# Four chained image layers on one Trainium2 core: where the table switches of Gelu and Silu may stand among the scan steps, and where the A matrices are loaded

## Chip, core and metric

The kernel runs on one core of one Trainium2 chip. The metric is the device time of one execution in microseconds (us); the lower, the better. All data is 32-bit float.

## What is computed

Eight images of 56 x 56 pixels with 192 channels go through four layers. Layer 0 has a convolution branch on one half of the channels and a state-space branch on the other; layers 1 and 2 are state-space layers; layer 3 is windowed attention with an MLP. Cut to what matters here:

```python
# layer 0: left half                       # right half
xl = relu(conv1x1(conv3x3(conv3x3(xl))))   xz = layernorm(xr) @ in_proj
                                           u  = silu(depthwise3x3(xz[:192])); gate = silu(xz[192:])
# layers 0, 1, 2: for each of 4 directions k over the 3136 pixels
dts, B, C = split(x_proj[k] @ u)           # rank 6 or 12, 16, 16 rows
delta = softplus(dt_proj[k] @ dts + bias)
A = -exp(A_logs)                           # [4, 192, 16]
h = exp(delta[d] * A[d, n]) * h + delta[d] * u[d] * B[n]     # 192 x 16 states, one recurrence each
y[d] = sum_n h[d, n] * C[n]                # summed over directions, plus D * u; then a layernorm
# layer 3: 7x7 windows, 6 heads: attention, layernorm, x1; then
out = x1 + layernorm(gelu(x1 @ fc1 + b1) @ fc2 + b2)
```

## The kernel before, in words

**The scans.** A step is one recurrence of 128 rows (32 channels x 4 states) over 784 pixels. One pass of one direction over a quarter of an image is a unit of 24 steps: two channel halves of 12 steps, each 4 groups of states x 3 groups of channels. There are 8 images x 3 layers x 4 directions x 4 quarters = 384 units, so 9216 steps; an image has 1152. In step s the loop in `run` emits:

- on ScalarE the exponential of step s, `ps_x = exp(dsp * A)`, into one of two PSUM buffers (`make`); A is used as the scale, one column per step. Ahead of it stands a copy of the last column of step s-2 into `state`;
- on GpSimd the product `db = usp * bt` of step s;
- on VectorE the scan of step s-1 and, for three steps of four, the product with `ct` into `hc`. Where s-1 is 3 mod 4 the scan writes `hc` and GpSimd makes the product one step later, so VectorE has a shorter step and GpSimd a longer one;
- on TensorE, for every third step, the sums over states into `ps_y` (`add_up`). At s = 5 mod 12 the finished half is copied out of `ps_y` by ScalarE (`merge`).

**Work ahead and work beside.** Three queues of Python generators are polled at the end of each step; only the head of a queue runs, and a `yield n` makes it wait n steps. `ahead` holds `prepare`: for a half that starts 13 steps later it makes two matmuls into both spare PSUM banks, then the softplus on ScalarE (with `table_time` before it), a product on GpSimd and six loads through SyncE's DMA queue. `urgent` holds `after` and `columns` (layernorms and projections between layers). `back` holds, for each image in this order, `ssm_front` of the next image (7 bands, Silu), `attention_block` of the previous image (8 rows of windows, one Gelu each) and `conv_front` of the next. After the `ahead` queue is polled, pieces of `urgent` and then of `back` are emitted as long as a budget of TensorE and ScalarE time per step (`SPARE`, at most `MOST`) is positive. `need` runs all queues with `forced` set until a named piece is done; it is what runs the prologue. Two PSUM banks serve all of this work (`bank`, `all_banks`). Each engine runs its instructions in exactly the order in which they were emitted (`in_order`).

**Tables.** Softplus, Gelu and Silu each need another activation table than the exponentials. Each use is a table load, the function, and a load back (`use_ln_exp`, line 390). `table_time` (line 393) lets such a use in only at steps 1 or 2 mod 4, unless forced.

**A.** In `constants` (lines 252 to 270) each layer's A is fetched by 16 DMAs that GpSimd issues (line 264), then ScalarE takes the exponential (line 268) and VectorE the negative (line 269). The queue of SyncE carries nearly all other transfers.

Of the kernel before, what the change touches and what calls it, by code (L numbers as in the profile page):

```python
# [32 lines left out]
AF = mybir.ActivationFunctionType  # L33
# [19 lines left out]
NSG = N // SN  # L53
NG = C // G * NSG
# [84 lines left out]
class Net:  # L139
# [56 lines left out]
    def constants(self, ctx):  # L196
        nc, cp = self.nc, self.cp
        self.vt = self.const("vec", [CH, NV])
        self.ident = cp.tile([128, 128], F32, name="ident")
        make_identity(nc, self.ident)  # L200
        self.ones = cp.tile([CH, CH], F32, name="ones")
        nc.vector.memset(self.ones, 1.0)
        self.eps = cp.tile([128, 1], F32, name="eps")
        nc.vector.memset(self.eps, EPS)
        self.blk = self.const("blk", [CH, CH])
        self.esum = cp.tile([128, G], F32, name="esum")
        nc.vector.reduce_sum(
            self.esum, self.ident.rearrange("p (d n) -> p d n", n=SN), axis=AX.X
        )


        self.wx = []
        for l in range(3):
            R = RANK[l]
            wx = cp.tile([CH, 2, 2, 4 * N + 2 * R], F32, name=f"wx{l}")
            for k in range(K):
                d, at = k // 2, 4 * N + k // 2 * R
                src = self.a[f"wx{l}"][:, :, k, :]
                nc.sync.dma_start(
                    out=wx[:, :, k % 2, 2 * N * d : 2 * N * d + 2 * N], in_=src[:, :, R:]  # L220
                )
                nc.scalar.dma_start(out=wx[:, :, k % 2, at : at + R], in_=src[:, :, :R])
                for c in range(2):
                    at = VAT[f"dtb{l}"] + c * K + k
                    nc.gpsimd.dma_start(
                        out=self.dtw[:1, l, k, CH * c : CH * c + CH],
                        in_=self.a["vec"][:, at : at + 1].rearrange("p o -> o p"),
                    )
            self.wx.append(wx)
            nc.sync.dma_start(out=self.dtw[1 : 1 + R, l], in_=self.a[f"dtw{l}"])  # L230

        with self.tc.tile_pool(name="setup", bufs=1) as sp:

            rstd = sp.tile([CH, 3], F32, name="rstd")
            at = VAT["bn1_v"]
            nc.scalar.activation(rstd, self.vt[:, at : at + 3], AF.Sqrt, bias=self.eps[:CH])
            nc.vector.reciprocal(rstd, rstd)
            self.bns = cp.tile([CH, 3], F32, name="bns")
            self.bnb = cp.tile([CH, 3], F32, name="bnb")
            at = VAT["bn1_g"]  # L240
            nc.vector.tensor_mul(self.bns, self.vt[:, at : at + 3], rstd)
            t = sp.tile([CH, 3], F32, name="bnt")
            at = VAT["bn1_m"]
            nc.vector.tensor_copy(t, self.vt[:, at : at + 3])
            for i in (1, 2):
                nc.vector.tensor_sub(t[:, i : i + 1], t[:, i : i + 1], self.v(f"conv{i}_b"))
            nc.vector.tensor_mul(t, t, self.bns)
            at = VAT["bn1_b"]
            nc.vector.tensor_sub(self.bnb, self.vt[:, at : at + 3], t)


            self.dsum = dsum = cp.tile([CH, 3, 2], F32, name="dsum")
            self.A = []
            for l in range(3):
                at = VAT[f"D{l}"]
                d = self.vt[:, at : at + 2 * K].rearrange("p (c k) -> p c k", k=K)
                nc.vector.reduce_sum(dsum[:, l, :], d, axis=AX.X)
                A = cp.tile([128, K, C // G, NSG], F32, name=f"A{l}")
                src = self.a[f"A{l}"].rearrange(
                    "(d s n) (k j q) -> q s d n k j", s=NSG, n=SN, k=K, q=4  # L260
                )
                for q in range(4):
                    for sg in range(NSG):
                        nc.gpsimd.dma_start(
                            out=A[32 * q : 32 * q + 32, :, :, sg], in_=src[q, sg]
                        )
                A = A.rearrange("p k j s -> p (k j s)")
                nc.scalar.activation(A, A, AF.Exp)
                nc.vector.tensor_scalar_mul(A, A, -1.0)
                self.A.append(A)  # L270


            ls = sp.tile([CH, 2], F32, name="ls")
            at = VAT["ls"]
            nc.vector.tensor_scalar_min(ls, self.vt[:, at : at + 2], math.log(100.0))
            nc.scalar.activation(ls, ls, AF.Exp)
            self.scm = cp.tile([CH, 2, 3], F32, name="scm")
            at = VAT["hm"]
            for c in range(2):
                nc.vector.tensor_scalar_mul(  # L280
                    self.scm[:, c, :], self.vt[:, at : at + 3], ls[:, c : c + 1]
                )
            self.ln1024 = cp.tile([CH, 1], F32, name="ln1024")
            nc.vector.memset(self.ln1024, 10.0 * math.log(2.0))

    def l3_constants(self):

# [105 lines left out]
    def table_time(self):  # L393


        while self.step % 4 not in (1, 2) and not self.forced:
            yield 1

    def other_table(self, func, *tiles):
# [415 lines left out]
    def run(self):  # L815
        nc = self.nc
# [13 lines left out]
        for i in range(NC):  # L830
            self.urgent.append(Task(self.after(-1, i)))
        self.urgent.append(Task(self.columns(0)))
        self.state = self.s1.tile([128, NG], F32, name="state")
        self.B_, self.C_, self.spread = {}, {}, {}

# [2 lines left out]
        ]  # L838
        S = len(steps)
        half = NG // 2  # L840
        self.step = 0
        self.ahead.append(Task(self.prepare(units[0], 0, 0)))
        self.need(("half", 0))
        self.ahead.append(Task(self.prepare(units[0], 1, half)))
        for sg in range(NSG):
            self.load_bc(units[0], sg)
        made, weighed, copies = {}, {}, deque()
        left = dict.fromkeys(self.load, 0.0)
        for s in range(S + 8):
# [5 lines left out]
            t = s + half + 1  # L855
            if t < S and t % half == 0:
                self.ahead.append(Task(self.prepare(*steps[t][:2], t)))
            if s < S and s % half == 0:
                self.need(("half", s))
                U = steps[s][0]  # L860
                if s % (16 * NG) == 0:
                    if U.l == 0:
                        self.begin_image(U.b)
                    self.dd = self.s1.tile([CH, 2, CH], F32, name="dd")
                    for c in range(2):
                        nc.scalar.activation(
                            self.dd[:, c, :], self.ident[:CH, :CH], AF.Copy,
                            scale=self.dsum[:, U.l, c : c + 1],
                        )

            t = s - 2
            if 0 <= t < S and not steps[t][0].last:
                U, h, sg, j = steps[t]
# [5 lines left out]
            t = s - 1  # L879
            if 0 <= t < S:  # L880
                U, h, sg, j = steps[t]
                x, db = made[t]
                pool = t % 4 == 3
                hc = self.s6.tile([128, CK], F32, name="hc")
                hs = hc if pool else x
                sense = slice(None) if U.k < 2 else slice(None, None, -1)
                nc.vector.tensor_tensor_scan(
                    hs[:, sense], x[:, sense], db[:, sense],
                    0.0 if U.first else self.at_state(h, sg, j), ALU.mult, ALU.add,
                )  # L890
                if not pool:
                    nc.vector.tensor_mul(hc, hs, self.C_[U, sg])
                made[t] = hs
                weighed[t] = hc
            t = s - 2
            if 0 <= t < S and t % 4 == 3:
                U, h, sg, j = steps[t]
                nc.gpsimd.tensor_mul(weighed[t], weighed[t], self.C_[U, sg])
            t = s - 4
            if 0 <= t < S and t % 3 == 2:  # L900
                U, h, sg, j = steps[t]
# [6 lines left out]
            while self.piece(self.ahead):  # L908
                pass
            self.spend(left, before)  # L910
            for queue in (self.urgent, self.back):
                while min(left["PE"], left["ACT"]) > 0.0 and self.piece(queue):
                    before = self.spend(left, before)

            t = s - 4
            if 0 <= t < S and t % NG >= half and t % 3 == 2:
                n = t // NG + 1
# [484 lines left out]
MOST = {"PE": 3.4, "ACT": 2.5, "DVE": 1.6, "POOL": 3.0}  # L1402


def view(t, k, c, i, n):

    if k % 2 == 0:
        return t[:, c, i : i + n]
    return t.rearrange("p c (h w) -> p c w h", w=HW)[:, c, i // HW : (i + n) // HW, :]
# [120 lines left out]
```

## Time and profile before

| | |
|---|---|
| median of 3 runs | 27071.03 us (27067.4 to 27074.87) |
| the profiled execution, its own time | 27060.61 us |
| its span, first to last instruction | 27058.8 us |
| VectorE (DVE) busy | 24122.4 us, 89% |
| GpSimd (POOL) busy | 23054.4 us, 85% |
| ScalarE (ACT) busy | 17211.8 us, 64% |
| TensorE (PE) busy | 18495.3 us, 68% |
| table loads | 1793 of 1.283 us |

Lines of the profile name engine, operation, output and input tiles, count, busy time and the idle time before the instructions with what ended it. Where the order was written out by hand most instructions carry line 109, so tiles tell them apart: `ps_x<-dsp,A` is a step's exponential, `TENSOR_TENSOR_SCAN` its scan, `db<-usp,bt` GpSimd's product, `delta<-ps_p` the softplus, `hid<-hid` the Gelu, `uband<-uband` and `sz<-sz` the Silu, `act<-ps_y` the merge copy. A line `ACT_TABLE_LOAD` with L109 or L268 goes to another table, one with L390 back.

### The profile page before, as it was taken

To read this page: it belongs to the slowest core of one execution; us is meant where nothing else is said; L and a number is where in the kernel's file an instruction comes from. 1 tells how busy PE (TensorE), PEld (TensorE's weight loads), DVE (VectorE), ACT (ScalarE), POOL (GpSimd) and SP (SyncE) were. 2 spreads that over 40 slices of the span, in tenths; PEclk is the share of its full clock that TensorE was granted. 3 is DMA by queue.
4 is the path that set the end of the run, shared out by engine and by line. 5 is a ranking of instruction groups with operands and counts; after the bars stand their busy time and mean duration, and the time that the engine had idled before them with its cause. 6 is when DMAs were issued, how large, how long until landed. Compare 5 with 4: busy or idle time off the path is not lost. (4 is left out here: it accounts for less than half of the span.)

```text
span 27058.8 us, 260255 instructions
## 1 busy us (share of the span) xinstructions
PE 18495.3 (68%) x76788; PEld 6432.0 (24%) x76788; DVE 24122.4 (89%) x18972; ACT 17211.8 (64%) x30893; POOL 23054.4 (85%) x13199
## 2 busy tenths in 40 slices
PE   6675567676676666766667676677766776676657
PEld 2221122222222222222222222222212222222114
DVE  5999999999999899999999999989999899999991
ACT  4655566665666666666666666666666666666655
POOL 5888988888888888888888888888888888888991
PEclk7776677777777777777777777777777777777777
DMA  4555565556555565555655556555565555555550
GB/s 96 135 138 124 133 136 133 126 127 139 135 132 127 125 144 132 132 126 129 142 131 132 127 131 140 133 129 127 131 140 131 129 128 135 134 129 129 130 132 25
DMA packets 1503447, 3472.21 MB, mean 128 GB/s; under 512 B 310618, under 2 KB 503219, under 8 KB 1502020
## 3 DMA queue, kind: packets, MB, share of 16 engines
q1 hardware_dynamic: 1496452, 3455.15, 56.0%
q8 instruction: 606, 9.93, 0.1%
q0 software_dynamic: 3072, 0.31, 0.1%
q14 instruction: 821, 6.73, 0.1%
q10 hardware_dynamic: 2496, 0.09, 0.0%
HBM read 1457.23 MB, written 147.89 MB: 59 GB/s over the span
## 5 line engine op out<-in xcount | busy, mean ns | idle before, releaser
L109 POOL TENSOR_TENSOR db<-usp,bt 128x784 f32<-128x784 f32 x9216 | 16832.7, 1857 | 161.8 <-DMA usp<-du 129.3
L109 DVE TENSOR_TENSOR_SCAN ps_x<-ps_x,state,db 128x784 f32<-128x784 f32 x5184 | 9569.7, 1846 | 834.0 <-ACT state L109 358.7
L109 ACT ACTIVATE ps_x<-dsp,A 128x784 f32<-128x784 f32 x9216 | 8464.1, 919 | 2496.9 <-DVE hc L109 2190.5
L109 PE MATMUL ps_y<-hc,esum 128*32 128x392 f32 x36864 | 6959.3, 641 | 1147.3 <-POOL hc L109 780.6
L109 DVE TENSOR_TENSOR hc<-ps_x,ct 128x784 f32<-128x784 f32 x6912 | 6739.5, 975 | 651.4 <-DVE ps_x L109 11.0
L109 POOL TENSOR_TENSOR hc<-hc,ct 128x784 f32<-128x784 f32 x2304 | 4254.4, 1847 | 2696.2 <-ACT state L109 2104.5
L109 ACT COPY state<-ps_x 128x1 f32<-128x1 f32 x5184 | 831.4, 160 | 4659.5 <-DVE hc L109 4637.4
L109 DVE TENSOR_TENSOR_SCAN hc<-ps_x,state,db 128x784 f32<-128x784 f32 x1728 | 3181.7, 1841 | 161.6 <-POOL db L109 58.2
L109 DVE TENSOR_TENSOR_SCAN ps_x<-ps_x,db 128x784 f32<-128x784 f32 x1728 | 3085.0, 1785 | 261.1 <-ACT state L109 149.1
L109 PEld LDWEIGHTS ps_y<-hc,esum 128*32 128x32 f32 x36864 | 1630.6, 130 | 6096.7 <-issue 3212.3
L109 PE MATMUL ps_y<-act,ident 96*96 96x392 f32 x2304 | 1612.2, 835 | 1760.4 <-ACT act L109 1746.4
L109 PE MATMUL ps_p<-act,act 13*96 13x392 f32 (+1 forms) x3072 | 1513.0, 605 | 1116.6 <-ACT s L109 210.4
L109 POOL TENSOR_TENSOR du<-delta,act 96x784 f32<-96x784 f32 x768 | 1567.9, 2042 | 201.3 <-ACT delta L109 198.7
L109 PE MATMUL ps_p<-act,wx 96*88 96x392 f32 (+1 forms) x1536 | 985.8, 778 | 686.9 <-ACT delta L109 394.0
L109 ACT ACT_TABLE_LOAD x896 | 1149.6, 1283 | 34.4 <-PE ps_p L109 18.9
L390 ACT ACT_TABLE_LOAD x897 | 1150.9, 1283 | 15.6
L109 PEld LDWEIGHTS ps_y<-act,ident 96*96 96x96 f32 x2304 | 465.0, 223 | 2603.1 <-ACT act L109 2056.6
L109 DVE TENSOR_TENSOR_SCAN hc<-ps_x,db 128x784 f32<-128x784 f32 x576 | 1025.8, 1781 | 58.8 <-ACT state L109 38.0
L109 PEld LDWEIGHTS ps_p<-act,act 13*96 13x96 f32 (+1 forms) x3072 | 465.4, 180 | 2033.6 <-issue 373.5
L109 ACT COPY act<-ps_y 96x784 f32<-96x784 f32 x768 | 928.0, 1208 | 8.5 <-PE ps_y L109 8.5
L109 PE MATMUL ps_p<-xip,diag 96*96 96x448 f32 x2016 | 864.0, 580 | 94.4 <-ACT delta L109 94.3
L109 ACT COPY state<-hc 128x1 f32<-128x1 f32 x1728 | 328.6, 190 | 883.6 <-DVE hc L109 880.4
(212 smaller groups left out, 18126.0 us busy)
## 6 DMA issues: line engine op xcount, KB each, us to landing
dsp<-delta SPq DMA_DIRECT2D x2304, 392.0 KB
usp<-du SPq DMA_DIRECT2D x2304, 392.0 KB
bt<-bcd SPq DMA_DIRECT2D x1536, 392.0 KB
ct<-bcd SPq DMA_DIRECT2D x1536, 392.0 KB
wf<-in_wf SPq DMA_DIRECT2D x128, 288.0 KB
wf<-wf2d SPq DMA_DIRECT2D x128, 288.0 KB
bcd<-bcx SPq DMA_DIRECT2D x256, 134.8 KB
szd<-sz SPq DMA_DIRECT2D x56, 336.0 KB
```

Source lines behind the costliest of these rows:

```text
L109: return call(out, *args, **k)
L390: self.tc.nc.scalar.preload_act_table_set(LN_EXP)
```

## The change

`table_time` now tells the softplus (queue `ahead`) from the others. Both still wait for steps at which neither this step nor the one before is 3 mod 4; beside that, nobody may start at 5 mod 12, and Gelu and Silu not at 0, 1 and 2 mod 12 either. So the softplus may stand at 1, 2, 6, 9 or 10 mod 12, Gelu and Silu at 6, 9 or 10. While a softplus waits, `urgent` and `back` emit nothing in that step (`quiet`); after a step in which Gelu or Silu waited, `back` is polled ahead of `urgent` (`wanted`). The A of layer 0 is fetched by ScalarE's DMA queue in the prologue, and its exponential comes after the first half has been prepared; those of layers 1 and 2 are fetched by SyncE and worked on in tasks at the end of the first `urgent` queue. `products` only gives a name to an expression that was there.

```diff
--- before.py
+++ after.py
@@ -250,24 +250,22 @@
 
 
             self.dsum = dsum = cp.tile([CH, 3, 2], F32, name="dsum")
-            self.A = []
+            self.A, self.logs = [], []
             for l in range(3):
                 at = VAT[f"D{l}"]
                 d = self.vt[:, at : at + 2 * K].rearrange("p (c k) -> p c k", k=K)
                 nc.vector.reduce_sum(dsum[:, l, :], d, axis=AX.X)
                 A = cp.tile([128, K, C // G, NSG], F32, name=f"A{l}")
+                self.A.append(A.rearrange("p k j s -> p (k j s)"))
                 src = self.a[f"A{l}"].rearrange(
                     "(d s n) (k j q) -> q s d n k j", s=NSG, n=SN, k=K, q=4
                 )
-                for q in range(4):
-                    for sg in range(NSG):
-                        nc.gpsimd.dma_start(
-                            out=A[32 * q : 32 * q + 32, :, :, sg], in_=src[q, sg]
-                        )
-                A = A.rearrange("p k j s -> p (k j s)")
-                nc.scalar.activation(A, A, AF.Exp)
-                nc.vector.tensor_scalar_mul(A, A, -1.0)
-                self.A.append(A)
+                self.logs.append([
+                    (A[32 * q : 32 * q + 32, :, :, sg], src[q, sg])
+                    for q in range(4) for sg in range(NSG)
+                ])
+            for out, part in self.logs[0]:
+                nc.scalar.dma_start(out=out, in_=part)
 
 
             ls = sp.tile([CH, 2], F32, name="ls")
@@ -282,6 +280,20 @@
                 )
             self.ln1024 = cp.tile([CH, 1], F32, name="ln1024")
             nc.vector.memset(self.ln1024, 10.0 * math.log(2.0))
+
+    def decay(self, l):
+
+        self.nc.scalar.activation(self.A[l], self.A[l], AF.Exp)
+        self.nc.vector.tensor_scalar_mul(self.A[l], self.A[l], -1.0)
+        self.done.add(("A", l))
+
+    def decays(self, l):
+        for n, (out, part) in enumerate(self.logs[l]):
+            self.nc.sync.dma_start(out=out, in_=part)
+            if n % 4 == 3:
+                yield 1
+        yield 4
+        self.decay(l)
 
     def l3_constants(self):
 
@@ -393,7 +405,18 @@
     def table_time(self):
 
 
-        while self.step % 4 not in (1, 2) and not self.forced:
+
+        ahead = self.rank == 2
+
+        def clear(s):
+            late = s % (NG // 2) == 5 or not ahead and s % (NG // 2) < 3
+            return not (late or products(s) or products(s - 1))
+
+        while not self.forced and not clear(self.step):
+            if ahead:
+                self.quiet = self.step
+            else:
+                self.wanted = self.step
             yield 1
 
     def other_table(self, func, *tiles):
@@ -830,6 +853,8 @@
         for i in range(NC):
             self.urgent.append(Task(self.after(-1, i)))
         self.urgent.append(Task(self.columns(0)))
+        for l in (1, 2):
+            self.urgent.append(Task(self.decays(l)))
         self.state = self.s1.tile([128, NG], F32, name="state")
         self.B_, self.C_, self.spread = {}, {}, {}
 
@@ -838,9 +863,10 @@
         ]
         S = len(steps)
         half = NG // 2
-        self.step = 0
+        self.step, self.quiet, self.wanted = 0, -1, -1
         self.ahead.append(Task(self.prepare(units[0], 0, 0)))
         self.need(("half", 0))
+        self.decay(0)
         self.ahead.append(Task(self.prepare(units[0], 1, half)))
         for sg in range(NSG):
             self.load_bc(units[0], sg)
@@ -859,6 +885,7 @@
                 self.need(("half", s))
                 U = steps[s][0]
                 if s % (16 * NG) == 0:
+                    self.need(("A", U.l))
                     if U.l == 0:
                         self.begin_image(U.b)
                     self.dd = self.s1.tile([CH, 2, CH], F32, name="dd")
@@ -880,7 +907,7 @@
             if 0 <= t < S:
                 U, h, sg, j = steps[t]
                 x, db = made[t]
-                pool = t % 4 == 3
+                pool = products(t)
                 hc = self.s6.tile([128, CK], F32, name="hc")
                 hs = hc if pool else x
                 sense = slice(None) if U.k < 2 else slice(None, None, -1)
@@ -893,7 +920,7 @@
                 made[t] = hs
                 weighed[t] = hc
             t = s - 2
-            if 0 <= t < S and t % 4 == 3:
+            if 0 <= t < S and products(t):
                 U, h, sg, j = steps[t]
                 nc.gpsimd.tensor_mul(weighed[t], weighed[t], self.C_[U, sg])
             t = s - 4
@@ -908,8 +935,9 @@
             while self.piece(self.ahead):
                 pass
             self.spend(left, before)
-            for queue in (self.urgent, self.back):
-                while min(left["PE"], left["ACT"]) > 0.0 and self.piece(queue):
+            both = self.urgent, self.back
+            for queue in both[::-1] if self.wanted == s - 1 else both:
+                while min(left["PE"], left["ACT"]) > 0.0 and self.quiet < s and self.piece(queue):
                     before = self.spend(left, before)
 
             t = s - 4
@@ -1402,6 +1430,11 @@
 MOST = {"PE": 3.4, "ACT": 2.5, "DVE": 1.6, "POOL": 3.0}
 
 
+def products(t):
+
+    return t % 4 == 3
+
+
 def view(t, k, c, i, n):
 
     if k % 2 == 0:
```

## Prediction

> **What bounds the kernel now.** I read the page's shares first, then two windows of equal length, one where no work lies beside the scans (last image, attention of the image before done) and one with attention beside them.
>
> ```profile
> PE 18495.3 (68%) x76788; PEld 6432.0 (24%) x76788; DVE 24122.4 (89%) x18972; ACT 17211.8 (64%) x30893; POOL 23054.4 (85%) x13199
> ```
> ```profile
> 25500.00:26300.00 800.00, 446.29 (x1473) 113.71 (x1472) 774.12 (x555) 449.04 (x693) 756.17 (x414) 0.69 0.58 132
> 10900.00:11700.00 800.00, 574.79 (x2584) 212.49 (x2585) 719.80 (x581) 529.41 (x1003) 690.54 (x400) 0.76 0.57 130
> ```
>
> The third number group with a count is DVE. Without other work it is 97% busy and a step is DVE's: four steps take three starts of 2.83 us and one of 1.76, 10.25 us. So 9216 steps cost 2304 x 10.25 = 23,616 us. From the first scan to the last the trace has 26,228, so 2612 us are lost. DVE's other work in that stretch, summed from the timeline, is 1343. The rest, about 1270, is waiting; some 145 of the 2612 fall in the first 100 steps. Softplus switches as such cost next to nothing: in the quiet stretch a half of 12 steps loses 0.49 us, one softplus included. With other work beside, a half loses 3 us. The page's groups tell whom DVE waits for:
>
> ```profile
> L109 DVE TENSOR_TENSOR_SCAN ps_x<-ps_x,state,db 128x784 f32<-128x784 f32 x5184 | 9569.7, 1846 | 834.0 <-ACT state L109 358.7
> L109 ACT ACT_TABLE_LOAD x896 | 1149.6, 1283 | 34.4 <-PE ps_p L109 18.9
> L390 ACT ACT_TABLE_LOAD x897 | 1150.9, 1283 | 15.6
> ```
>
> It is ScalarE, idle a third of the time but late where a block of its own stands in its order. One Gelu at 5 mod 12, from the timeline of ACT and of DVE:
>
> ```profile
> 11419.33 0.81 ACT L109 COPY act<-ps_y 96x784 f32<-96x784 f32 x1
> 11421.24 1.28 ACT L109 ACT_TABLE_LOAD   x1
> 11422.54 2.17 ACT L109 ACTIVATE hid<-hid 128x2352 f32<-128x2352 f32 x1
> 11424.72 1.28 ACT L390 ACT_TABLE_LOAD   x1
> 11426.01 1.76 ACT L109 ACTIVATE ps_x<-dsp,A 128x784 f32<-128x784 f32 x2
> ...
> 11427.04 1.86 DVE L109 TENSOR_TENSOR_SCAN ps_x<-ps_x,state,db 128x784 f32<-128x784 f32 x1 [4.59 <-ACT ps_x L109]
> ```
>
> Merge copy, other copies, then 4.76 us of switch: the next exponential comes late and the scan waits 4.59 us. The prologue, on ACT:
>
> ```profile
> 10.51 0.30 ACT L236 ACTIVATE rstd<-vec,eps 96x3 f32<-96x3 f32 x1
> 33.57 1.28 ACT L268 ACT_TABLE_LOAD   x1 [22.76 <-DMA A<-in_A]
> 47.75 0.28 ACT L268 ACTIVATE A<-A 128x96 f32<-128x96 f32 x1 [12.61 <-DMA A<-in_A]
> 63.22 0.28 ACT L268 ACTIVATE A<-A 128x96 f32<-128x96 f32 x1 [15.18 <-DMA A<-in_A]
> 64.08 1.28 ACT L390 ACT_TABLE_LOAD   x1
> 65.37 4.91 ACT L109 ACTIVATE diag<-ident,wdw 96x96 f32<-96x96 f32 x18
> ```
>
> ACT stands for A until 63.2 us; everything up to the first scan at 181.1 us follows from the line at 65.37 in one chain.
>
> **The Trainium skill.** "ScalarE: Activation LUTs", What ACT_TABLE_LOAD costs, gives 1283 ns for a load and about 1380 ns of drain. The load agrees (1283); the drain doesn't show: a softplus with both loads takes 3.47 us from load to load, of which 2.57 is loads and 0.88 softplus. "DMA: Bandwidth & Descriptors", Issuing engines are not separate DMA queues, says that another issuing engine saves only issue time. Here it is the issue that counts: the 48 A transfers take GpSimd 46.7 us to issue (0.98 each). The same page, Rules for kernel authors, says that a strided last dimension becomes a descriptor per element; A's runs are strided, so its issue from ACT or SyncE is an unseen form. No run shows it; my bounds are below.
>
> **The change, part by part.** To price a switch I walked through the trace, put each switch to the step of the last exponential before it, and gave it every DVE wait over 0.1 us that it overlaps or that begins within 1.5 us after it. That gives (count x mean = us):
>
> - Gelu at 5: 22 x 5.1 = 112; at 2 (behind a softplus at 1): 18 x 2.8 = 50; at 9: 16 x 2.1 = 34. Together 196 (8 more are in the tail, forced).
> - Silu at 2: 28 x 2.3 = 64; at 9: 27 x 0.6 = 16. Together 80.
> - Softplus at 5: 81 x 1.3 = 106; at 1: 642 x 0.21 = 134; at 2: 43 x 0.33 = 14.
>
> (1) *Gelu* moves to 6, 9 or 10. Step 6 isn't in the trace. From rows: exponential 0.92 + state copy 0.16 + switch 4.76 + next state copy and exponential 1.08 = 6.9 us, against two full steps of 5.66 that two PSUM buffers allow: at least 1.2. The dearest comparable place is step 2 with its softplus, 2.8. I take the measured 2.1 of step 9: 56 x 2.1 = 118, **saves 78** (bounds: 67 at 1.2, so 129; 157 at 2.8, so 39).
> (2) *Silu* (4.3 us, 3.5 without the second tile) the same way: 55 x 0.6 = 33, **saves 47** (0 if they cost 1.45 as now; 80 if nothing).
> (3) *Softplus 5 to 6*, clear of the copy (0.81 above): 0.92 + 0.16 + 3.47 + 1.08 = 5.63 us, just within 5.66. At step 1 it costs 0.21: 81 x 0.2 = 16, **saves 90** (0 to 106). It holds both banks a step longer. Its loads are due from step 9 mod 12 of a half 13 steps ahead, so nothing later is late.
> (4) *Prologue.* The 48 issues leave GpSimd. ACT issues 16 after line 236, behind its 12 of wx (8.43 us, 0.6 to 0.7 each). At 0.6 to 1.0 each (POOL's row above) that is 10 to 16 us from 10.8, then the load for `exp(ls)` 1.28 + 0.20 + load back 1.28: `diag` starts at 24 to 30 instead of 65.4. Its other inputs are earlier: SyncE issues wdw and the tokens by 15.6, GpSimd's 24 issues end at 13.9. **Saves 38** (35 to 41). Removed with it: two exponentials (0.28) and negatives (0.21), which stood in these waits. A's first exponential and negative now stand ahead of the first scan: 0.5.
> (5) *A of layers 1 and 2.* 32 DMAs pass through SyncE, four per step, about 19 us at wx's 0.60 on SyncE, in 8 steps of 23 us; SyncE issues for 37% of the time (10.0 ms in sum), so loads behind it may be some 5 us late; they are issued 3 to 5 steps (8 to 14 us) ahead, and that hides it. I take 5 (0 to 20). Two exponentials and negatives in some step near 60 to 80: 1. They are needed at step 384.
> (6) *`quiet`.* At 0 mod 12, where a softplus that is ready early waits for 1, `urgent` and `back` stay silent. What is withheld is emitted later; softplus has both banks then, so most of it couldn't run anyway. I take 0: the gain is at most the 134 of softplus at 1 plus some 15 of its neighbours, the loss at most what rival E tells. The extra waits of Gelu and Silu (0 to 7 steps, 2.6 on average over all residues, against 0.75 now: under 2 more, 15 times an image) make `back` some 30 steps longer, `quiet` up to a twelfth. `back` has room: in images 1 to 6 its last row is written at step 1059 of 1152, and its product is wanted only some 288 steps into the next image; in the last image it ends at step 665.
> (7) *`wanted`* lets Gelu go ahead of `urgent` at its step: 0, since `urgent` has quarters of an image of lead.
>
> Everything that Gelu and Silu shift re-deals which step holds which other work; for that I give back 10. Sum: 78 + 47 + 90 + 38 - 5 - 2 - 10 = **236 us** off 27,060.6, the profiled execution's own time: 26,825. The median of the runs lies 10.4 above it, so 26,835.
>
> **What is late next.** DVE's waits outside any switch: 537 us for ScalarE, most where it stands idle behind a TensorE result for other work (worst ahead of scan 8 mod 12, 319 us), 202 for GpSimd and 125 for TensorE, 864 in all. The change doesn't aim at these.
>
> **Rivals.** A, the forecast: 26,740 to 26,930, chance 0.55.
> B, *more*: `quiet` clears ScalarE ahead of softplus at 1 too, another 134 + 15: 26,686, chance 0.10. For it: the quiet stretch, where softplus is nearly free. Against: the banks were taken anyway.
> C, *half*: Gelu at 6 stands behind the drained merge copy and costs 4 (-106), softplus at 6 costs 0.5 (-24): 26,965, chance 0.15. For it: the copy sometimes takes 1.6 us as it waits.
> D, *the prologue alone*: the scheduling gains (about 200) are eaten by re-dealt work, 27,033, chance 0.10. The same time results if the wait at 5 is hardly ever met.
> E, *slower*: the other work comes in denser bursts, since softplus keeps both banks from about step 2 to 6 and Gelu keeps the head of `back` for up to 7 steps; ScalarE, in order, stands more often behind a matmul that is queued. Place: the 864 us of waits outside switches. At 27% more (236) the gain is gone, at 37% more the time is 26,835 + 0.37 x 864 = 27,155. For it: 319 us of this sort already fall on one residue. Against: the amount of work is the same and the budget per step too. Chance 0.10.
>
> **How the numbers follow.** A measurement of this kernel can tell about 0.2% (54 us) from no change: 27,017 to 27,125. A, B and C are faster, 0.80; D is the same, 0.10; E slower, 0.10. The range 26,690 to 27,050 takes in A, C and D's time and the bounds of (1) to (6); outside are most of E and D's upper part, and half of B.
>
> **What would show it.** No switch at 5 mod 12 outside forced places, no Gelu or Silu at 2; Gelu at 6 or 9 with a DVE wait near 2.1 us; first scan near 143 us and no A rows on line 264; DVE's busy time unchanged (24,122 less 0) while its idle time shrinks by some 230; the last image's `back` later than step 665 but before 1152, and the tail of 650 us after the last scan (26,408) as it was. The prediction is wrong if waits ahead of scans without a switch nearby grow by over 100 us, if softplus at 6 shows waits over 1 us, or if the scans stall where an image begins because `back` isn't done.

## The result, and the profile after

| | before | after |
|---|---|---|
| median of 5 runs each | 27071.03 us (27045.79 to 27077.22) | 27214.14 us (27200.07 to 27228.64) |
| ratio, 95% interval | | 1.0054 [1.0039, 1.0068] |
| profiled execution, its span | 27058.8 us | 27198.3 us |
| first scan | 181.14 us | 143.84 us |
| first scan to end of the last | 26,229 us | 26,399 us |
| last scan to the end | 648 us | 656 us |

The change made the kernel slower by 143 us, where 236 us of gain were forecast. In the two profiled executions the difference of 139.5 us is -37.3 ahead of the first scan, +169.1 among the scans and +7.7 behind them. So the loss lies wholly among the scans, where the gain was expected. The page of after, engines and two groups:

```profile
PE 18550.7 (68%) x76788; PEld 6441.8 (24%) x76788; DVE 24117.6 (89%) x18972; ACT 17212.2 (63%) x30893; POOL 22999.0 (85%) x13151
...
L109 DVE TENSOR_TENSOR_SCAN ps_x<-ps_x,state,db 128x784 f32<-128x784 f32 x5184 | 9568.4, 1846 | 659.4 <-ACT ps_x L109 299.7
...
L109 PE MATMUL ps_p<-act,wx 96*88 96x392 f32 (+1 forms) x1536 | 981.9, 775 | 862.1 <-DMA act<-u0d 528.6
```

VectorE does the same work (24,117.6 us against 24,122.4), as forecast. The idle time ahead of the commonest scans even fell, from 834.0 to 659.4. What grew is in the last line: TensorE now stands (idles, with this as its next instruction) 528.6 us for one load, `act<-u0d`, ahead of the projection; before it was 224.4. The two windows of the prediction again, whose third group is VectorE:

```profile
25500.00:26300.00 800.00, 456.52 (x1494) 115.52 (x1492) 770.05 (x549) 448.76 (x685) 750.35 (x412) 0.69 0.58 133
10900.00:11700.00 800.00, 580.27 (x2633) 215.73 (x2632) 724.90 (x585) 533.55 (x1016) 696.21 (x404) 0.77 0.58 130
```

In the middle of an image, beside attention, VectorE is a little busier than before (724.90 of 800 us against 719.80; the windows don't hold quite the same steps). So nothing is lost in this stretch; the loss has to be looked for elsewhere.

To find it I took every wait of VectorE over 0.15 us from the start of the first scan to the last scan and put it to a cause: a table switch that it overlaps or follows within 1.5 us; else, where the release came from ScalarE, the longest stand of ScalarE just ahead of it and the matmul that this waited for. Sums in us, for the kernels named further down too:

| cause of VectorE's wait | before | after | not silenced | gap | softplus alone | Gelu alone |
|---|---|---|---|---|---|---|
| switch for softplus | 265 | 177 | 177 | 158 | 173 | 251 |
| switch for Gelu | 197 | 101 | 118 | 121 | 184 | 89 |
| switch for Silu | 179 | 117 | 125 | 125 | 181 | 178 |
| ACT behind projection `act,wx` | 58 | **262** | 54 | 80 | 57 | 64 |
| ACT behind `xb,wqkv` | 46 | **117** | 45 | 115 | 42 | 51 |
| ACT behind norm sums `bsq,ones` | 0 | **145** | 88 | 110 | 0 | 60 |
| ACT behind expand `xb,wf` | 96 | 37 | 123 | 19 | 104 | 148 |
| all the rest | 670 | 733 | 699 | 768 | 685 | 648 |
| sum | 1511 | 1688 | 1429 | 1496 | 1426 | 1490 |

(The sums are rounded by themselves.) The switches did what was expected of them: 641 us fell to 395, by 246 where steps (1) to (3) said 215. Waits outside switches rose from 870 to 1294, by 424. That is nearly the whole case: +177 of waits, and the scans take 169 longer.

**The largest of them.** The list of waits of before (total us, times, longest):

```profile
PE ps_p L109 <- DMA act<-u0d: 224.4, 25, 13.4
ACT bcx L109 <- PE ps_p L109: 216.2, 121, 11.2
```

and the same of after:

```profile
PE ps_p L109 <- DMA act<-u0d: 528.6, 31, 21.7
ACT bcx L109 <- PE ps_p L109: 513.7, 133, 13.1
PE ps_p L109 <- DMA xb<-u3d: 300.1, 40, 13.1
```

A count of VectorE's single waits over 6 us among the scans finds 12 before and 39 after. The new ones are 28 at steps 16, 1095 or 1096, 1120 and 1144 of an image, seven of each (an eighth time no next image's `u0` is loaded), of 9 to 11 us, 276 in all. (Six of them stand in the row "all the rest", since there VectorE waits for TensorE itself.) One of them in the timeline of after (start, duration, engine; SPq are DMA issues of SyncE):

```profile
13277.38 0.88 ACT L109 ACTIVATE delta<-ps_p 96x392 f32<-96x392 f32 x2
...
13278.29 0.55 SPq L1049 DMA_DIRECT2D dsp<-delta  x1
...
13280.83 0.54 SPq L1049 DMA_DIRECT2D usp<-du  x1
13281.43 4.14 SPq L759 DMA_DIRECT2D u3d<-aux  x2
13285.61 0.62 SPq L736 DMA_DIRECT2D act<-u0d  x1
...
13291.42 2.86 PE L109 MATMUL ps_p<-act,wx 96*76 96x392 f32 x4 [17.02 <-DMA act<-u0d]
...
13294.32 0.48 ACT L109 COPY bcx<-ps_p 76x392 f32<-76x392 f32 x1 [12.60 <-PE ps_p L109]
...
13295.78 1.86 DVE L109 TENSOR_TENSOR_SCAN ps_x<-ps_x,state,db 128x784 f32<-128x784 f32 x1 [10.30 <-ACT state L109]
```

and the same work before:

```profile
13242.59 1.48 SPq L736 DMA_DIRECT2D u3d<-aux  x2
13244.16 0.58 SPq L713 DMA_DIRECT2D act<-u0d  x1
...
13247.45 0.88 ACT L109 ACTIVATE delta<-ps_p 96x392 f32<-96x392 f32 x2
...
13248.35 1.28 ACT L390 ACT_TABLE_LOAD   x1
...
13250.34 2.87 PE L109 MATMUL ps_p<-act,wx 96*76 96x392 f32 x4 [8.64 <-DMA act<-u0d]
...
13253.24 0.48 ACT L109 COPY bcx<-ps_p 76x392 f32<-76x392 f32 x1 [1.32 <-PE ps_p L109]
```

It is the task `after` of `urgent`, where one image ends and the next begins: it stores the finished tokens (`u3d<-aux`), loads the next image's `u0` into `act`, and with no `yield` between, emits the projection that reads it. Before, the stores and the load are issued 3 to 5 us ahead of the softplus. After, `urgent` is silent at step 0 mod 12, so they are emitted at step 1, behind the softplus and its two loads `dsp` and `usp`. SyncE issues in order: it waits for the softplus, then for GpSimd's `du`, and the load starts 8 us after the softplus began instead of 3 ahead of it. TensorE, in order, stands 17.0 us at the projection, ScalarE 12.6 at the copy behind it, the exponentials queue behind that, and the scan waits 10.3. Before, the copy behind TensorE's stand of 8.64 us waited only 1.32: the softplus and its two table loads lay ahead of it on ScalarE. The stand itself was there before in every image that has a next one: TensorE stood 7.4 to 10.3 us for this load at 22 places before, and in nearly all of them the next scans waited 1.1 us at most.

### The profile page after: what moved, and what is told of

It is laid out like the page before. It is cut to its first block, busy times and chain, and to the rows that moved or that the text cites. A ratio compares the mean times of both kernels' runs of the same rounds, so it can differ in the third digit from the quotient of the medians.

```text
span 27198.3 us, 260287 instructions
## 1 busy us (share of the span) xinstructions
PE 18550.7 (68%) x76788; PEld 6441.8 (24%) x76788; DVE 24117.6 (89%) x18972; ACT 17212.2 (63%) x30893; POOL 22999.0 (85%) x13151
## 5 line engine op out<-in xcount | busy, mean ns | idle before, releaser
L109 DVE TENSOR_TENSOR_SCAN ps_x<-ps_x,state,db 128x784 f32<-128x784 f32 x5184 | 9568.4, 1846 | 659.4 <-ACT ps_x L109 299.7
L109 PE MATMUL ps_p<-act,wx 96*88 96x392 f32 (+1 forms) x1536 | 981.9, 775 | 862.1 <-DMA act<-u0d 528.6
L109 PE MATMUL ps_p<-xb,wqkv 96*96 96x392 f32 x936 | 541.7, 734 | 512.7 <-DMA xb<-u3d 300.1
```

The costliest lines, as they stand in the source:

```text
L109: return call(out, *args, **k)
```

## The experiments

Each ratio is to the kernel before, timed on the same chip. Differences in us are between medians; between experiments they can be of two chips, and the median of before lay between 27,057 and 27,071 us.

**1. Not silenced.** The changed kernel without the silence:

```diff
-                while min(left["PE"], left["ACT"]) > 0.0 and self.quiet < s and self.piece(queue):
+                while min(left["PE"], left["ACT"]) > 0.0 and self.piece(queue):
```

> The changed kernel, but `urgent` and `back` are also polled in a step in which a softplus waits. Theory Q (the silent step puts the stores of u3d and the load of the next image's u0 behind the softplus's loads in SyncE's order, and TensorE, then ScalarE, stand until that load lands: four waits of 9 to 10 us an image in seven images, against about 1 each before): some 240 us less than the changed kernel, near 26,975, and those four waits back at about 1 us. Theory P (the new places of Gelu and Silu, and a conv_front that ends later, bring the loss): within 40 us of the changed kernel's 27,214, the four waits still there.

Measured: 26969.95 us (26947.62 to 26973.16), 0.9966 [0.9953, 0.9978]. One clause of the change costs 244 us by the medians (27,214 - 26,970; some 238 by the ratios); without it the rest is a gain of 0.34%. Its waits:

```profile
PE ps_p L109 <- DMA act<-u0d: 228.9, 26, 13.5
ACT bcx L109 <- PE ps_p L109: 194.9, 105, 11.3
PE ps_p L109 <- DMA xb<-u3d: 174.6, 31, 13.1
```

The first two are back at the numbers of before (224.4 and 216.2), and no wait over 6 us is left at the four places. The granted TensorE clock doesn't explain the loss: it was 0.751 in the profiled execution of after, 0.753 here, and 0.749 in that of experiment 12, some 250 us faster than after. Nor did the silence buy anything where step (6) saw a possible gain: the waits at the softplus's switches are 177 us with it and 177 without.

**2. Silence without the new places.** The changed kernel with `quiet` and `wanted`, all three functions in the places of before:

```diff
-            late = s % (NG // 2) == 5 or not ahead and s % (NG // 2) < 3
-            return not (late or products(s) or products(s - 1))
+            return not (products(s) or products(s - 1))
```

> The changed kernel with the places of before (any step 1 or 2 mod 4), silent step and queue order kept. Theory Q: the four waits an image stay, so 240 us over the A moves alone: near 27,270. Theory P: no new waits, near 27,034.

Measured: 27232.99 us (27223.0 to 27245.42), 1.0065 [1.0051, 1.0078]. The four waits per image are all there, and TensorE's stand for `act<-u0d` sums to 598.2 us. So the silence needs none of the new places to do its harm. (The moved A and `wanted` are still in this kernel; A alone gives 27,044, in experiment 10.)

**3. The gap.** The changed kernel, silence and all, with time between the load and the projection:

```diff
                     out=self.bufs[(g + 1) % 2][:, :, at], in_=self.u0[b + 1][:, :, at]
                 )
+                yield 6
             self.done.add(("u3", b, i))
```

> The changed kernel, silent step kept, but the task waits six steps between the load of the next image's u0 and the projection that reads it. Theory Q (the loss is TensorE standing in its order for that load): the four waits of 9 to 10 us an image vanish, near 26,975, as without the silent step. Rival R (the loss comes from what the silent step withholds, whatever stands behind the load): near 27,214.

Measured: 27043.98 us (27025.83 to 27064.86), 0.9992 [0.9984, 1.0001].

```profile
PE ps_p L109 <- DMA act<-u0d: 26.8, 5, 13.7
PE ps_p L109 <- DMA xb<-u3d: 328.4, 40, 13.3
```

The late load, not the silence as such, makes the four waits: given six steps, TensorE stands 26.8 us for it instead of 528.6, no wait over 6 us is left at the four places, and 170 us come back. The gap by itself is no gain: where nothing is silenced it gives none (experiment 12). The expectation had set all of the silence's cost on this load; some 74 of 244 us are elsewhere. The second line stays, 328.4 us: TensorE standing for attention's window load `xb<-u3d` (24.1 before, 174.6 in experiment 1, 300.1 after).

**4. `back` silenced alone.** The changed kernel with

```diff
-                while min(left["PE"], left["ACT"]) > 0.0 and self.quiet < s and self.piece(queue):
+                while min(left["PE"], left["ACT"]) > 0.0 and (self.quiet < s or queue is self.urgent) and self.piece(queue):
```

> The changed kernel, but only `back` is silent where a softplus waits; `urgent` is polled. Theory Q (it is `urgent` that is pushed behind the softplus's loads): near 26,970 and no four waits. Rival R (fewer steps for `back`, denser bursts): near 27,214.

Measured: 27059.22 us (27043.74 to 27085.8), 1.0000 [0.9992, 1.0008], 155 us less than with both silent and 89 more than with neither.

```profile
PE ps_p L109 <- DMA act<-u0d: 342.5, 31, 17.2
PE ps_p L109 <- DMA xb<-u3d: 295.9, 40, 13.4
```

The waits at steps 16 and 1144 are gone, those at 1095 and 1120 are still there in six images. In one of them the load is again issued behind the stores late after a softplus, and TensorE stands 16.91 us for it. There `conv_front` of the next image is still at work, up to step 1125 of 1152 (1059 before). So I expected too much of it: a delayed `back` reaches into the end of the image. That it is `conv_front`'s late work which holds up the load there is read from the order in the trace; it was not tried apart.

**5. The new places alone.** The kernel before, with nothing silenced, A as before, and in `table_time`

```diff
-        while self.step % 4 not in (1, 2) and not self.forced:
+        ahead = self.rank == 2
+
+        def clear(s):
+            late = s % (NG // 2) == 5 or not ahead and s % (NG // 2) < 3
+            return not late and s % 4 in (1, 2)
+
+        while not self.forced and not clear(self.step):
```

> The kernel before with the new places alone (never 5 mod 12; Gelu and Silu not at 0 to 2 mod 12); no silent step, no queue order, A as before. Theory Q: the switches save about 240 us of DVE waits; the waits of DVE behind the MLP's norm, which the fixed place of Gelu brings to the same residue each time, cost up to 200: 26,850 to 27,050, and no waits of 9 us for u0. Theory P: the loss is here, near 27,250.

Measured: 26990.24 us (26968.07 to 27004.01), 0.9974 [0.9963, 0.9985]. The placing itself pays, 68 us by the medians instead of the forecast's 205 (78 + 47 + 90 - 10).

**6. Softplus alone, and 7. Gelu and Silu alone.** Experiment 5 with the first added line for 6, the second for 7:

```diff
-            late = s % (NG // 2) == 5 or not ahead and s % (NG // 2) < 3
+            late = ahead and s % (NG // 2) == 5
...
+            late = not ahead and s % (NG // 2) in (0, 1, 2, 5)
```

> The kernel before (27,058 in the runs so far), with the softplus alone kept off 5 mod 12. The forecast's term by itself: 90 us less, 26,968. Rival (the switches' waits go, but the work beside them takes the place): under 45 us less, 27,015 or more.

Measured: 26953.03 us (26938.88 to 26961.82), 0.9958 [0.9946, 0.9971].

> The kernel before, with Gelu and Silu alone kept off 0, 1, 2 and 5 mod 12. The forecast's terms by themselves: 125 us less, 26,933. Rival (the work beside takes the place): since both places together gave 68 us, between 20 and 60 less, 27,000 to 27,040.

Measured: 27035.24 us (27018.82 to 27054.18), 0.9989 [0.9983, 0.9996]. Keeping softplus off 5 gives 110 us, the other two 28, and both together (68) give less than softplus alone. By the medians, then, the places of Gelu and Silu don't add to the gain of softplus but take from it; the intervals of 5 and 6 overlap a little. By my count of the traces the Gelus outside the tail stand half at 6 and half at 9 mod 12 in experiment 7, and nearly all at 6 in the kernel after.

**8. Gelu alone.** Experiment 7 for Gelu only; `other_table` passes what it is about to call:

```diff
-            late = not ahead and s % (NG // 2) in (0, 1, 2, 5)
+            late = gelu and s % (NG // 2) in (0, 1, 2, 5)
...
-        yield from self.table_time()
+        yield from self.table_time(func == AF.Gelu)
```

> The kernel before with Gelu alone kept off 0, 1, 2 and 5 mod 12 (A, softplus, Silu as before, nothing silenced). In the run with Gelu and Silu both kept off, waits at their switches fell by 150 us in the trace but waits at expand (96 to 161), at the norm after the MLP (0 to 61) and at the projection (37 to 61) took most of it back, and only 28 us remained. Theory: a Gelu fixed to 6 mod 12 fixes the place of the rest of its row, so the norm wait (about 60) and most of the expand wait (some 30) come with Gelu: against 96 us won at Gelu switches some 20 remain, 27,040. Rival: the loss comes with Silu, whose 50 us were eaten by the expand wait, and Gelu alone is worth about 80: 26,980, with no norm wait.

Measured: 27041.42 us (27031.57 to 27053.59), 0.9994 [0.9986, 1.0002]. The list of waits of this kernel:

```profile
ACT hid L109 <- PE ps_p L109: 307.5, 228, 4.3
ACT ps_p L109 <- PE ps_p L109: 117.7, 61, 4.9
```

Before, these were 238.7 and 41.7. In the table Gelu's switches fall by 108, and the waits behind expand (+52) and behind the norm sums (+60) eat it. So the waits went where the theory of that expectation said: Gelu is worth 15 us, with an interval that takes in none, and Silu with it 28. How the second wait looks is seen in the changed kernel, in the timelines of ScalarE and of VectorE: a Gelu at 6 mod 12, after which a scan waits 2.89 us, and 38 us later the norm of the same row, behind TensorE:

```profile
11467.11 2.17 ACT L109 ACTIVATE hid<-hid 128x2352 f32<-128x2352 f32 x1
...
11505.40 0.56 ACT L109 ACTIVATE ps_p<-ps_p,eps 96x392 f32<-96x392 f32 x1 [4.77 <-PE ps_p L109]
```
```profile
11471.79 1.79 DVE L109 TENSOR_TENSOR_SCAN hc<-ps_x,db 128x784 f32<-128x784 f32 x1 [2.89 <-ACT state L109]
...
11506.50 1.03 DVE L109 TENSOR_TENSOR proj<-ps_p,proj 96x392 f32<-96x392 f32 x2 [4.23 <-ACT ps_p L109]
```

**9. The norm moved.** Experiment 1, and in the MLP between Gelu and the second product

```diff
-        yield 1
+        yield 5
```

> The changed kernel with nothing silenced for the softplus, and after a Gelu a pause of 5 steps instead of 1 before the second product of the MLP. Theory: Gelu always at 6 mod 12 puts the sums of the norm where TensorE has a block of its own ahead of them, and ScalarE stands there (88 us in the trace without the pause); moved by four steps this wait falls below 40 and the time is some 50 us under that without the pause: about 26,920. Rival: the waits are made by the mass of other work per step and only change places; the norm wait falls, others rise by as much: 26,970.

Measured: 26961.69 us (26947.11 to 26982.47), 0.9966 [0.9952, 0.9979]: no gain over experiment 1. Its waits:

```profile
ACT bcx L109 <- PE ps_p L109: 275.1, 106, 11.3
ACT proj L109 <- PE ps_p L109: 237.6, 104, 9.3
ACT ps_p L109 <- PE ps_p L109: 33.4, 50, 1.9
```

In experiment 1 these three are 194.9, 143.7 and 153.5. The norm wait goes, as the theory said (in VectorE's waits 88 to 1), and its rival is right on the time: the waits behind `act,wx` (54 to 128), behind MLP's second product (25 to 76) and at softplus (177 to 225) take its place; six waits over 6 us appear at step 1097.

**10. A alone.** Loads and exponentials of A moved as in the change's diff (`constants`, `decay`, `decays` and the three places in `run` that call or need them), all else as in the kernel before.

> The A moves of the change alone; the places of softplus, Gelu and Silu, and the order of the queues, are those of before. Both theories: 37 us less than before (the first scan at 144 instead of 181 us), so about 27,034, and the stretch of the scans unchanged.

Measured: 27043.51 us (27029.86 to 27058.1), 0.9995 [0.9987, 1.0003]. The first scan is at 144.3 us, 37 earlier, but only some 15 us are left in the time, and the interval takes in none. The prologue of after on ScalarE:

```profile
11.68 14.05 ACTq L268 DMA_DIRECT2D A<-in_A  x16
25.76 1.28 ACT L274 ACT_TABLE_LOAD   x1 [15.41 <-DMA win<-in_win]
27.27 1.28 ACT L402 ACT_TABLE_LOAD   x1
28.57 4.91 ACT L109 ACTIVATE diag<-ident,wdw 96x96 f32<-96x96 f32 x18
```

`diag` starts at 28.6 us, inside the 24 to 30 of step (4). The loss comes at the halves of steps 84 to 107: they take 81.7 us where they took 64.2. There A1 and A2 are issued by SyncE. From the timeline of this kernel:

```profile
530.12 7.34 SPq L292 DMA_DIRECT2D A<-in_A  x8
537.55 0.65 SPq L1048 DMA_DIRECT2D usp<-du  x1
538.31 0.60 SPq L1048 DMA_DIRECT2D dsp<-delta  x1
```
```profile
544.75 0.92 ACT L109 ACTIVATE ps_x<-dsp,A 128x784 f32<-128x784 f32 x1 [6.56 <-DMA dsp<-delta]
```

The 32 issues take 36.6 us between 490 and 538 us, 1.14 each, in the same stretch in which the softplus's loads are due; `dsp` lands so late that ScalarE waits 6.56 us for it (5.61 and 3.47 at two other places), and the scan behind it 4.02. That A1's and A2's loads are the cause is read from this order; a kernel with them elsewhere was not run. Nor do the runs tell the time of the issues from the transfers themselves: these 32 are 24,832 packets (last section).

**11. The two parts that pay, and 12. these with the gap.** Experiment 10 with the place of softplus from experiment 6; then also with the `yield 6` of experiment 3.

```diff
-            return not (products(s) or products(s - 1))
+            late = ahead and s % (NG // 2) == 5
+            return not (late or products(s) or products(s - 1))
```

> Only the two parts that paid alone, together: the softplus kept off 5 mod 12, and the moved A. Gelu and Silu in the places of before, nothing silenced, order of the queues as before. Alone they gave about 108 and 19 us, so if they add: 26,940. Rival: the moved A shifts all that comes later by some steps, and the two parts overlap at the start; then no more than the softplus alone, 26,955 to 26,970.

Measured: 26930.42 us (26927.26 to 26941.05), 0.9954 [0.9942, 0.9967]. By the medians the parts add (110 + 15, and 126 under the kernel before on the same chip), and this is the lowest median of all; but the interval of softplus alone, 0.9958 [0.9946, 0.9971], is nearly the same, so what A adds isn't clear of the noise.

> The kernel of soft_and_A with 6 steps between the load of the next image's u0 and the projection that reads it. With the softplus not silencing anything this load is rarely late (ScalarE stood some 58 us in all for this product in the kernel before): theory, it gains 10 to 40 us, 26,900 to 26,930. Rival: the pause costs as much as it gains, since the urgent queue ends later: 26,940 or more.

Measured: 26944.2 us (26939.38 to 26950.88), 0.9959 [0.9946, 0.9971]: the rival's side. Where nothing is silenced the gap gains nothing; 14 us are lost by the medians, which the intervals don't tell from none. So the 170 us of experiment 3 come from the late load and not from a gap that would pay anywhere.

## Why the prediction was wrong

**The step that failed is (6),** "I take 0", with its reason: "What is withheld is emitted later; softplus has both banks then, so most of it couldn't run anyway". Its true price is 244 us, and it turns the forecast around: 236 of gain would have been about 90, and are -143. Two things were wrong in the reason. What is withheld isn't only work for banks: it holds DMA issues. And "later" means behind the softplus in every in-order queue, SyncE's among them, whose next instructions wait for the softplus and for GpSimd. I had counted the queues passed for A, step (5), and not for work that stays where it is while the softplus is put in front of it. The trace of before shows the danger: 22 stands of TensorE for `act<-u0d`, of 7.4 to 10.3 us, covered by where they fell (in the one shown, while ScalarE was at the softplus and its table loads). (The longest of its list, 13.4, is another case: it lies at step 12, at the very start, and the scans did wait for it.) Of the 244 us, 170 come back when this load has time (experiment 3). With `back` alone silent 89 us are lost, part of them to the same load at two of the four places (experiment 4). TensorE's stand for the window load `xb<-u3d` comes with `back` being silent, 295.9 us in experiment 4 and 300.1 after against 174.6 in experiment 1, and VectorE's waits behind `xb,wqkv` are 117 after against 45; how much of the other 74 us this makes was not separated.

**Rival E**, given a chance of 0.10, had the sign and the kind, ScalarE in its order behind a matmul, in "the 864 us of waits outside switches". By my count these rose by 424 us, or 49%, where the prediction had named over 100 us as a sign of being wrong; E's formula with 0.49 gives 26,835 + 423 = 27,258, near the 27,214 measured. The nearness is in part luck, since the gains at the switches were not those of the sum either (246 against 215). E's mechanism was only half right: it looked for denser bursts everywhere, and over half of the new waits (the 276 us at 28 places) are one late load. **Rival B** had hoped for more from the silence at softplus's switches; nothing of that shows (177 us with and without it).

**Steps (1) and (2)**, Gelu and Silu, 78 + 47 = 125: the price of a switch was right (after, the Gelus at 6 mod 12 cost 1.9 us each by my count, forecast 2.1), and the waits at the switches fell by 150 (experiment 7), but the time only by 28. My sum counted only the waits at the moved instruction. Each of them stands inside a chain of tasks; fixing one of them at one or two of twelve places fixes the places of those behind it, which had been spread before. What I gave back for this, 10 us of "re-dealt" work, was the mis-sized term; it is about 120. Experiment 9 shows that moving the next link only moves the wait.

**Step (3)**, softplus off 5, said 90 and gave 110 [79, 146 by its interval]. The argument was right: behind the copy of the merge a switch doesn't fit two steps, and at 6 it does; VectorE's waits at softplus's switches fell by 92 (265 to 173), most of the gain. That it held because the softplus's results have slack and nothing else in its chain moves is my reading, not a test.

**Step (4)**, 38 ahead of the first scan: 37.3. **Step (5)**, 5 + 1 (0 to 20), is some 17 in the stretch of experiment 10, near the end of its bounds: I priced the issue at 0.60 each from `wx`, while A's took 1.14, and took for hidden what delays `dsp`. The `dsp` of experiment 10's lines is issued 6.4 us ahead of the exponential that waits for it; the same one was issued 9.8 us ahead before. **Step (7)** was not tried alone; experiment 1 is experiment 5 with A moved and `wanted`, and it is 20 us below it, about what A gives, so 0 fits.

## What to carry to other kernels

Holding back background work for a few microseconds isn't free when it issues DMAs: ask in every in-order queue what comes to stand in front of it, and look for consumers emitted right behind their load. The trace of before lists such consumers already, as long waits that cost nothing yet. And when a step inside a chain of tasks is pinned to one phase of a periodic schedule, price the phases of its successors too; move by itself what has slack, as I take it that the softplus has.

## What the runs showed of the hardware

A's strided loads took longer to issue than `dsp` and `usp`: a median of 0.77 us on ScalarE's queue and 0.85 on SyncE's in the kernel after (one took 3.30), against 0.55 for `dsp` and `usp` on SyncE's, and 0.98 for the same loads on GpSimd's before. They aren't the dearest: `ct`'s loads took 1.95 on SyncE's queue, a median too. The prediction cited the Trainium skill ("DMA: Bandwidth & Descriptors", Issuing engines are not separate DMA queues) for issue time as all that another issuer saves; the runs add the size of it: 0.98 us each on GpSimd in the prologue of before, 0.88 on ScalarE in the prologue of after (14.05 us for 16), 1.14 among the scans on SyncE in experiment 10 (36.6 us for 32). Engine and place change together here, so the runs don't say which makes the difference.

The prediction also left open what the strided form becomes on another queue. The pages of before and of experiment 10 show it (queue, packets, MB):

```profile
q1 hardware_dynamic: 1496452, 3455.15, 56.0%
q0 software_dynamic: 3072, 0.31, 0.1%
q10 hardware_dynamic: 2496, 0.09, 0.0%
```
```profile
q1 hardware_dynamic: 1521284, 3455.25, 56.1%
q10 hardware_dynamic: 14912, 0.14, 0.0%
q0 software_dynamic: 768, 0.01, 0.0%
```

The 48 loads were 2304 packets on GpSimd's queue, 48 each. The 16 that went to ScalarE's queue (q10) are 12,416 packets and the 32 on SyncE's (q1) 24,832, so 776 each: one for every element of a load (32 x 24 = 768), and 8 more. So another issuer changed the packets too, and not only the issue time.
